# Moving v's projections to the end of a half step, with a query-key projection in their place

## The chip, the cores and the metric

The kernel runs on one core of a Trainium2 chip. TensorE (PE) does the matrix products and the transposes, VectorE (DVE), ScalarE (ACT) and GpSimd (POOL) the elementwise work, and SyncE (SP) issues nearly all DMA transfers. The metric is the time of one execution in microseconds (us), as the device counts it; the median of three runs before the change is 3634.91 us (3633.56 to 3640.62).

## The reference: what is computed

The input is 16 sequences of 256 tokens with 128 features, in float32. First comes one causal attention layer with 16 heads of 8 features, added to its input. Then come six layers, and what they make is added too:

```python
for i in range(DEPTH):                       # 6
    x = attn_layer(shift_tokens(x), ...) + x # 16 heads of 64, windows of 32
    x = ffn_layer(shift_tokens(x), ...) + x  # layernorm, W1, a * gelu(gate), W2
```

`shift_tokens` moves half of the features one token on. `attn_layer` projects to q, k and v (1024 features each), divides q and k by their lengths per head, scales and rotates them by position, and lets each window of 32 queries attend to its own and the previous window, with a mask. The output is projected back to 128 features.

## The kernel before, in words

A first stage (up to about 390 us) does the causal attention; it is not touched. The second stage, lines 378 to 863, does the six layers and takes the rest.

The unit of the second stage is one sequence in one layer, n = 0 to 95 (six layers of 16 sequences; sequence n % 16). Every n is done in two **half steps**, `half(n, u)` with u = 0 and 1, and a half step mixes the work of several n, so that the engines have something to do while others finish:

- for n + 2: `shift` and the projections to q and k, `proj_qk(n + 2, g, k)`, for four groups g of heads, with k = 0 for q and 1 for k. In half u the groups are i = 2u and j = 2u + 1. Each projection is a pair of products on PE (name `qk`), a square on ACT (line 486, `sq`), a product with the position tables on DVE (line 487, `t`); after k = 1, three additions on POOL (lines 496 and 499, `sq` and `tq`).
- for n + 1: the lengths of q and k. In u = 0 `norms` sums the squares on PE (`n`), `roots` transposes them (`nT`) and takes the reciprocal root on DVE in a chain of small operations (lines 521 to 530, `nx`, `rn`, `nz`), and POOL spreads the result (line 533, `kb`). `spread_k` transposes kb on PE (line 544, `bc`), `norm_k` multiplies k with it on DVE (line 558, `tq`), and four DMAs on SP put q and k in place (`us`); both for two groups in u = 0 and two in u = 1.
- for n: `masks` and `sim` put the masked scores into PSUM (lines 585 and 605), `soften` scales them and subtracts their maximum (DVE `sm`, `mx`, POOL line 626), `power` takes the exponential (ACT line 632).
- for n (u = 1) or n - 1 (u = 0), the blocks bi and bj: `share` divides by the sum (DVE `rec`, POOL or DVE line 642), `attn_T` transposes the weights on PE (line 648, `aT`) with a copy on ACT, `attn_v` multiplies them with v in 64 small products on PE (line 668, `po`) with a copy on ACT (line 677, `ao`). `project_out` of n - 1 is `wo`.
- v: `proj_v(n, u, c)` projects the half c of the tokens for the heads of u: one product on PE (line 568, recorded as two), a copy on ACT (line 574, `vn`), and transfers on SP that lay v out a window further on (`vs`): two for c = 0 (lines 575 and 577), one for c = 1. It is read by `attn_v` in the half step that follows. On a layer's first sequence `load_v` fetches the weights.
- for the pair m of two sequences: the feed-forward part, spread over the half steps. In **odd n, u = 0** `glu_center` takes off the mean (PE `cen`, ACT line 709 `fsq` and line 711 `xc`) and `glu_var` sums the squares (PE line 718, `pv`, which reads fsq); in **odd n, u = 1** come `glu_norm` and two of three `glu_part` (PE `hg`, `ha`, ACT line 753, DVE line 755); in **even n, u = 0** the third; in **even n, u = 1** `glu_out` (PE `w`).

So there are four kinds of half steps, and a cycle of four repeats 48 times.

PSUM has four single buffers for all of this (`psum1`: qk, n, nT, aT, v, cen, pv, hg, ha, bc, wo, w take them in turn) and two double ones (`psum2`, for sim and po). A product waits until the earlier tenant of its buffer has been read.

The order of the work is the order in which the code calls it. `in_order` (line 89) ties every instruction of PE, DVE, ACT and POOL to the one before it on its engine; only SP's transfers are placed by the scheduler. Each engine then works through its queue in that order, and waits by semaphores where an input or a buffer isn't ready.

## Time and profile before

| | us |
|---|---|
| median of three runs | 3634.91 (3633.56 to 3640.62) |
| the profiled execution | 3631.49, of which the span is 3629.4 |
| PE busy | 3485.9 (96%), at a mean granted clock of 0.992 |
| DVE busy | 2841.1 (78%) |
| POOL busy | 2592.8 (71%) |
| ACT busy | 1870.2 (52%) |
| PE's share of the chain that ended last | 76% |

The profile is one execution. A line of a timeline gives the start in us from the span's start, the duration, the engine, the line of the code, the operation, what it writes and reads, how many instructions are merged in the row, and in brackets the idle time of the engine before it with what ended it. A line of the waits gives the engine and line that waited, for whom, the total, how often, and the longest. Two times are told apart by subtracting starts: on PE the end of a product is modelled and overlaps the next start, so the step from one start to the next is what counts.

### The profile page before, as it was taken

What the parts mean: (1) busy time and instruction counts of PE and PEld (TensorE: products, weight loads), DVE (VectorE), ACT (ScalarE), POOL (GpSimd) and SP (SyncE); (2) the same over time, 40 slices, a digit from 0 to 9 for tenths busy, and PEclk for the clock granted to TensorE, in tenths of its full rate; (3) what the DMA queues carried; (4) which work ended last, traced back from release to release, by engine and by line L of the source; (5) the groups of instructions that cost most, each with busy time, mean ns of one, the idle gap of its engine ahead of it and who ended that gap; (6) DMA issues with size and microseconds to landing.
All of it is one profiled execution on the core that took longest, in us unless ns stands there. A gap on an engine that the chain in (4) does not pass through costs nothing.

```text
span 3629.4 us, 153727 instructions
## 1 busy us (share of the span) xinstructions
PE 3485.9 (96%) x68032; PEld 2451.9 (68%) x68032; DVE 2841.1 (78%) x4866; ACT 1870.2 (52%) x3132; POOL 2592.8 (71%) x2731
## 2 busy tenths in 40 slices
PE   7999799999999999999999999999999999999998
PEld 5777466666666666666666666666676666666665
DVE  5765788887888888888877888877888888888784
ACT  2444355554555555555555555555555555555453
POOL 2221778778777778787777777778777877777772
PEclk9999899999999999999999999999999999999999
DMA  2000333334433334333334433334433343333342
GB/s 82 8 10 10 94 91 100 100 88 110 111 102 84 96 100 111 102 104 100 88 92 117 107 88 99 100 86 116 111 95 83 100 111 93 102 105 102 90 105 60
DMA packets 249444, 331.65 MB, mean 91 GB/s; under 512 B 74446, under 2 KB 105548, under 8 KB 247884
## 3 DMA queue, kind: packets, MB, share of 16 engines
q1 hardware_dynamic: 248060, 321.13, 33.1%
q8 instruction: 536, 8.78, 1.0%
q14 instruction: 128, 1.05, 0.1%
q10 hardware_dynamic: 720, 0.70, 0.1%
HBM read 28.12 MB, written 4.19 MB: 9 GB/s over the span
## 4 chain that ended last, share of the span: by engine, by line
PE 76%; DVE 9%; issue 7%; POOL 3%; ACT 2%; DMA 1%; SPq 0%; POOLq 0%; DVEq 0%; ACTq 0%
PE qk L485 17%; PE po L668 11%; PE v L568 9%; PE wo L688 8%; PE sim L605 6%; PE w L764 4%; PE hg L750 3%; PE ha L751 3%; PE aT L648 3%; PE n L506 2%; DVE tq L558 2%; DVE t L487 2%; PE bc L544 2%; PE sim L585 2%; ACT aT L650 1%
## 5 line engine op out<-in xcount | busy, mean ns | idle before, releaser
L487 DVE TENSOR_TENSOR t<-qk,ab 128x1024 f32<-128x1024 f32 x768 | 915.9, 1218 | 284.1 <-ACT sq L486 252.4
L499 POOL TENSOR_TENSOR tq<-t 128x512 f32<-128x512 f32 x768 | 962.1, 1274 | 85.4 <-DVE t L487 61.0
L485 PE MATMUL qk<-xs,wqk 128*128 128x256 f32 x3072 | 790.9, 393 | 1.6 <-DVE yT L693 1.5
L496 POOL TENSOR_TENSOR sq<-sq 128x512 f32<-128x512 f32 x384 | 489.1, 1274 | 282.3 <-ACT sq L486 272.3
L485 PEld LDWEIGHTS qk<-xs,wqk 128*128 128x128 f32 x3072 | 555.3, 191 | 146.9 <-issue 45.5
L486 ACT ACTIVATE sq<-qk 128x512 f32<-128x512 f32 x768 | 459.4, 599 | 377.3 <-PE qk L485 371.3
L650 ACT COPY aT<-aT 128x512 f32<-128x512 f32 x384 | 207.6, 587 | 599.4 <-PE aT L648 599.2
L668 PEld LDWEIGHTS po<-aT,vs 64*64 64x64 f32 x12288 | 327.8, 135 | 201.2 <-issue 106.8
L568 PE MATMUL v<-wv,xs 128*128 128x512 f32 x768 | 423.8, 634 | 28.1 <-ACT aT L650 21.2
L626 POOL TENSOR_TENSOR sm<-sm,mx 128x512 f32<-128x512 f32 x384 | 396.6, 1045 | 28.1 <-DVE mx L625 27.2
L605 PEld LDWEIGHTS sim<-us 64*32 64x32 f32 x24576 | 260.7, 105 | 205.9 <-issue 189.1
L668 PE MATMUL po<-aT,vs 64*64 64x32 f32 x12288 | 394.6, 222 | 5.2 <-issue 2.6
L668 PE MATMUL po<-aT,vn 64*64 64x32 f32 x12288 | 386.8, 219 | 4.6 <-issue 4.6
L574 ACT COPY vn<-v 128x512 f32<-128x512 f32 x384 | 225.3, 587 | 312.8 <-PE v L568 308.7
L688 PE MATMUL wo<-ao,wout 128*128 128x256 f32 x1536 | 383.2, 392 | 1.0 <-ACT ao L677 1.0
L642 POOL TENSOR_TENSOR ex<-ex,rec 128x512 f32<-128x512 f32 x288 | 317.5, 1116 | 39.7 <-ACT vn L574 18.2
L668 PEld LDWEIGHTS po<-aT,vn 64*64 64x64 f32 x12288 | 330.2, 136 | 5.1 <-issue 4.9
L605 PE MATMUL sim<-us 64*32 64x64 f32 (+1 forms) x24576 | 322.9, 221 | 3.1 <-DMA us<-tq 3.1
L688 PEld LDWEIGHTS wo<-ao,wout 128*128 128x128 f32 x1536 | 276.0, 189 | 49.5 <-ACT ao L677 1.7
L677 ACT COPY ao<-po 128x512 f32<-128x512 f32 x384 | 222.7, 580 | 114.9 <-PE po L668 114.9
L639 DVE TENSOR_REDUCE rec<-ex 128x8 f32<-128x512 f32 x384 | 252.0, 657 | 34.2 <-ACT ex L632 34.2
L625 DVE TENSOR_REDUCE mx<-sm 128x8 f32<-128x512 f32 x384 | 263.5, 686 | 13.3
(122 smaller groups left out, 5244.7 us busy)
## 6 DMA issues: line engine op xcount, KB each, us to landing
us<-tq SPq DMA_DIRECT2D x768, 256.0 KB
vs<-vn SPq DMA_DIRECT2D x384, 192.0 KB
vs<-vn SPq DMA_DIRECT2D x192, 64.0 KB
wqk<-in_f_wqkv_dram SPq DMA_DIRECT2D x96, 64.0 KB
ab<-in_tables_dram SPq DMA_DIRECT2D x6, 1024.0 KB
wv<-in_f_wqkv_dram SPq DMA_DIRECT2D x12, 256.0 KB
wout<-in_f_wo_dram SPq DMA_DIRECT2D x24, 128.0 KB
x<-in_x_dram SPq DMA_DIRECT2D x16, 128.0 KB
```

The lines of the kernel that those rows point to most:

```text
L485: nc.tensor.matmul(ps[:, t * S : t * S + S], W["qk", g][:, k, t, :], xs[n], start=True, stop=True)
L486: nc.scalar.activation(sq2[:, k].rearrange("p t n -> p (t n)"), ps, AF.Square)
L487: nc.vector.tensor_tensor(t12[:, k].rearrange("p f t n -> p f (t n)"), ps.unsqueeze(1).to_broadcast([P, 2, 2 * S]), W["ab", l][:, k].rearr ...
L496: nc.gpsimd.tensor_tensor(sq[n, g], sq2[:, :, 0, :], sq2[:, :, 1, :], ALU.add)
L499: nc.gpsimd.tensor_tensor(tq[n, g][:, t], t12[:, :, 0, t, :], t12[:, :, 1, 1 - t, :], ALU.add)
L568: nc.tensor.matmul(ps, xs[n][:, P * c : P * c + P], W["v"][:, u].rearrange("p g x d -> p (g x d)"), start=True, stop=True)
L605: nc.tensor.matmul(ps[WIN * r : WIN * r + WIN, x, col + first : col + 64], qk[part, g, 0, WIN * c : WIN * c + WIN], qk[part, g, 1, WIN * ( ...
L625: nc.vector.tensor_reduce(mx, seg, AX.X, ALU.max)
L626: nc.gpsimd.tensor_tensor(seg, seg, mx.unsqueeze(2).to_broadcast([P, 8, 64]), ALU.subtract)
L642: on.tensor_tensor(seg, seg, rec.unsqueeze(2).to_broadcast([P, 8, 64]), ALU.mult)
L668: nc.tensor.matmul(po[DH * y : DH * y + DH, h, x, g, WIN * r : WIN * r + WIN], v[64 * h : 64 * h + 64, r // 2, 2 * g + y, x, :], aT[64 * h ...
L688: nc.tensor.matmul(ps[:, :S].rearrange("p (h m) -> p h m", h=2), W["out"][:, g, 2 * u + x, :], a[:, x, :, g, :], start=(j == 0), stop=(j == 3)
```

## The change

Two calls in `half` change places. The first piece of v, `proj_v(n, u, 0)`, stood between the transposes `attn_T` and the values `attn_v(b, bi)`; it now stands at the end of the half step, directly ahead of the second piece. Where it stood, there is now the q projection of the second group, `proj_qk(n + 2, j, 0)`, which stood after `attn_v(b, bi)` (and in odd n, u = 0 after `glu_center`). Nothing is added or left out.

```diff
             do(b, attn_T, bi)
             do(b, attn_T, bj)
-            do(n, proj_v, u, 0)
+            do(n + 2, proj_qk, j, 0)
             do(b, attn_v, bi)
             if not even and u == 0 and glu(m):
                 glu_center(m)
-            do(n + 2, proj_qk, j, 0)
             if even and u == 0 and glu(m - 1):
                 glu_part(m - 1, 2)
...
                     leave(2 * ((m - 1) % 8))
                     leave(2 * ((m - 1) % 8) + 1)
+            do(n, proj_v, u, 0)
             do(n, proj_v, u, 1)
```

## The prediction

> **What bounds the kernel now.** I read the page's busy line first, then the stretches of 600 us, the waits of PE, and the timeline of each engine over one cycle of four half steps (2061 to 2127 us). Half steps (n, u) come in four kinds: u = 0 or 1, n even or odd.

> ```profile
> PE 3485.9 (96%) x68032; PEld 2451.9 (68%) x68032; DVE 2841.1 (78%) x4866; ACT 1870.2 (52%) x3132; POOL 2592.8 (71%) x2731
> ```
> ```profile
> 1450.00:2050.00 600.00, 590.61 (x11562) 411.86 (x11561) 489.76 (x812) 322.62 (x531) 470.94 (x490) 1.00 0.38 101
> ```

> In the long middle PE (first figure after 600.00) is busy 590.6 of 600 us at granted clock 1.00; DVE, ACT and POOL have 18%, 46% and 22% idle. PE takes its queue in order, so the time is PE's work plus each place where its next instruction is not ready. A cycle is 65.9 us. The change leaves PE the same instructions; only gaps can change. What gaps there are stand in the waits (us in total, times, longest):

> ```profile
> PE v L568 <- ACT aT L650: 21.2, 89, 0.2
> PE v L568 <- DVE tq L558: 6.1, 33, 0.4
> ```

> Now the two u = 0 kinds, from the timelines (start, duration, engine, line, idle before). Even n, PE, then DVE, then POOL:

> ```profile
> 2069.11 1.12 PE L568 MATMUL v<-wv,xs 128*128 128x512 f32 x2 [0.24 <-ACT aT L650]
> 2070.17 0.32 PE L668 MATMUL po<-aT,vs 64*64 64x32 f32 x8
> ...
> 2071.23 1.13 PE L485 MATMUL qk<-xs,wqk 128*128 128x256 f32 x4
> 2072.20 1.02 PE L750 MATMUL hg<-xn,w 128*85 128x512 f32 x2
> 2073.06 1.02 PE L751 MATMUL ha<-xn,w 128*85 128x512 f32 x2
> 2073.91 1.03 PE L485 MATMUL qk<-xs,wqk 128*128 128x256 f32 x4
> 2074.78 0.60 PE L544 MATMUL bc<-cst,kb 128*128 128x128 f32 x4
> ```
> ```profile
> 2063.96 2.36 DVE L487 TENSOR_TENSOR t<-qk,ab 128x1024 f32<-128x1024 f32 x2 [0.71 <-ACT sq L486]
> ...
> 2070.25 1.00 DVE L528 TENSOR_TENSOR nz<-nx,rn 128x64 f32<-128x64 f32 x1
> ```
> ```profile
> 2066.64 2.52 POOL L499 TENSOR_TENSOR tq<-t 128x512 f32<-128x512 f32 x2
> 2069.10 2.07 POOL L626 TENSOR_TENSOR sm<-sm,mx 128x512 f32<-128x512 f32 x2
> 2073.45 1.04 POOL L533 COPY kb<-rn 128x1024 f32<-128x1024 f32 x1 [2.29 <-DVE rn L530]
> ```

> bc reads kb, which POOL finishes at 2074.49; PE comes to bc at 2074.78. The slack is 0.29 us, hidden by work ahead of it. Odd n, PE, ACT, DVE and POOL:

> ```profile
> 2103.67 1.13 PE L707 MATMUL cen<-x,cst 128*128 128x512 f32 x2
> 2104.64 1.03 PE L485 MATMUL qk<-xs,wqk 128*128 128x256 f32 x4
> 2105.50 1.04 PE L718 MATMUL pv<-cst,fsq 128*128 128x1 f32 x8
> 2106.40 1.11 PE L485 MATMUL qk<-xs,wqk 128*128 128x256 f32 x4
> 2107.35 0.60 PE L544 MATMUL bc<-cst,kb 128*128 128x128 f32 x4
> ```
> ```profile
> 2104.84 0.60 ACT L709 ACTIVATE fsq<-cen 128x512 f32<-128x512 f32 x1 [0.44 <-PE cen L707]
> ```
> ```profile
> 2096.46 2.36 DVE L487 TENSOR_TENSOR t<-qk,ab 128x1024 f32<-128x1024 f32 x2 [1.08 <-ACT sq L486]
> ```
> ```profile
> 2105.70 1.04 POOL L533 COPY kb<-rn 128x1024 f32<-128x1024 f32 x1 [2.29 <-PE qk L485]
> ```

> pv reads fsq, which ends at 2105.44, and starts at 2105.50: the qk between cen and pv fills exactly the time of ACT's square. kb has 0.61 us of slack here (2106.74 against 2107.35).

> **The change, part by part.**

> *The projection qk(j,0) takes v's place after the transposes.* Its four matmuls go ahead of the 64 of attn_v(bi), on ACT its square ahead of the copy ao and, in odd u = 0, of fsq and xc; on DVE its t meets nothing new. It waits, as v did, for the first aT copy, so the 0.24 us stay. Price there: v to po is 1.06 us (2069.11 to 2070.17); qk is a matmul of the same pitch (0.86), so 1.06 again: nothing. At a layer's start its weight loads pass vs's transfers on SP, which makes them earlier.

> *Odd u = 0: qk leaves the place between cen and pv.* cen stays at 2103.67, fsq at 2104.84 to 2105.44, pv at 2105.50; PE stands idle for the 0.86 us that qk took. Behind pv are queued qk(j,1), bc, attn_v(bj), the masks and the next half. ACT is free for fsq (it waited 0.44 us for cen). So nothing becomes earlier, and v is added at the end of the half: v before another full matmul 0.97 (like qk to hg after po), the second v 0.95 (2092.81 to 2093.76 in even u = 1) in place of 1.05 (2109.28 to 2110.33): +0.87. The weight load that qk covered may now show for up to 0.1. I take 0.92 (bounds 0.75, if fsq comes 0.1 earlier, and 1.06) in the 46 odd steps that hold cen and a projection: 42.3 us.

> *Even u = 0: v leaves the stretch before bc.* PE would reach bc at 2069.11 + 1.06 + 1.06 + 0.97 + 0.86 + 0.86 = 2073.92. kb cannot follow: it ends a chain on DVE and POOL that starts with t at 2063.96, and that t waited 0.71 us for the square of a projection at the half's head, which does not move. One part can: DVE's first nz takes 1.00 us where the next two take 0.22, and ends at 2071.25, 0.08 after POOL's subtraction (2071.17); in odd n the two ends are 2103.48 and 2103.41. POOL's tq before it could start 0.2 earlier (t ends 2066.32, tq starts 2066.64 behind POOL's own queue, which the earlier projection of the half before shortens). So kb at 2074.29, bc at 2074.35: 0.43 earlier than now, v 0.87 at the end, 0.1 for a weight load no longer covered: +0.54. Bounds: 0.2 (kb 0.5 earlier) and 0.86 (kb unmoved, 0.63, and switches of 0.1 twice). 42 steps: 22.7 us. I take the value nearer the middle because both halves' rows tie nz's end to POOL's.

> [...]

> *Odd u = 1.* PE's order becomes qk, po, hg, ha, hg, ha, qk. ACT's first gelu ends at 2123.23; its table load began when the square was done and moves up some 1.1 us with qk, so the later qk, which needs its PSUM place, does not wait. v's two copies on ACT stand ahead of the next half's square: 0.59 more, covered by that same 1.1 us; without it the next square would be 0.32 late (0.27 idle before it now). Price 0.

> *Even u = 1.* attn_v(bj) now has one projection (0.96) between it and attn_v(bi), whose ao copy ends 0.73 after PE leaves it (2086.80 to 2087.53): no wait. The v that waited 0.18 us for DVE's tq becomes a qk that waits for the same; PE comes there later than DVE does now: the 6.1 us of the second wait line go.

> *v's transfers.* c = 0's two now stand on SP behind us's four (u = 0) and ahead of c = 1's: the last starts about 1.1 to 1.9 us later than 2080.64, and attn_v needs it at about 2086.3. The trace shows no landing; it shows no wait with 5.1 us and leaves about 3.5. Bounds 0 and 1 us at 94 steps; I take 0, since this stretch uses 0.62 of the DMA engines. v's weights (load_v), asked for on SP before the last vs of the half ahead, are needed only at the half's end: nothing.

> *Edges.* First and last even steps have kb with 0.05 of slack: 2 × 0.9. At five layer starts POOL's tables (L427) hold everything; POOL's queue ahead of them is 1.1 us earlier, against v's 0.87: 5 × -0.25.

> Sum: 42.3 + 22.7 - 6.1 + 1.8 - 1.3 = 59.4 us. The profiled execution took 3631.5 (span 3629.4), so 3690.9; the runs' median is 3.4 above it, so **3694**.

> **The rivals.**

> *Only pv's gap opens (0.12).* POOL and DVE run ahead far enough that kb comes 0.5 us earlier: 42.3 - 6.1 + 0.5 gives 3672. For it: the 22% that POOL has idle. Against: DVE waits for PE (0.71) at the chain's head.

> *Both gaps at their upper bounds (0.16).* 46 × 1.06 + 42 × 0.86 + 1.8 = 87 us and no gain: 3722. [...]

> *Transfers late (0.05).* 0.5 us at 94 steps more: 3741. For it: 0.62 of the DMA engines in that stretch; against: 3.5 us of room.

> *Not slower (0.05).* PE's records are pipelined and their ends modelled; if DVE's queue paces the halves (it runs without idle time from 2075.75 to 2087.53) and PE only looks full, v at the end and the gap before pv lie in PE's slack, and even u = 1's wait goes: 3629. It decides where DVE has less idle time at a half's head than the gap is long; the rows say 0.71 and 1.08, against 0.43 and 0.86.

> **How the numbers follow.** Main case 0.62 (3681 to 3708 by itself). 3668 to 3724 holds it, the first two rivals but their edges, some 0.87. A measurement here tells 0.2% (7 us) from nothing: slower 0.95; same 0.03 and faster 0.02 come from the last rival, whose 3629 lies near the edge.

> **What would show it.** After: a wait of PE pv on ACT fsq of 0.8 to 0.9 us some 46 times; PE bc on POOL kb of about 0.4, some 42 times; "v <- ACT aT" turned into "qk <- ACT aT", still 0.24; "<- DVE tq" gone; the cycle 67.2 us. Wrong if pv starts less than 1.7 us after cen, if kb ends more than 0.5 us earlier in its half, or if po waits for vs.

## The result, and the profile after

The changed kernel takes 3699.51 us (median of 4 executions, 3698.94 to 3701.81) against 3635.19 us before: a ratio of 1.0179, 95% interval 1.0166 to 1.0192, or 64 us more. The profiled execution took 3699.42 (span 3697.5) against 3631.49. The forecast was 3694.

The busy line of the page, and the stretch of the long middle that was shown of before:

```profile
PE 3508.1 (95%) x68032; PEld 2457.5 (66%) x68032; DVE 2845.4 (77%) x4866; ACT 1874.5 (51%) x3132; POOL 2577.3 (70%) x2731
```
```profile
1450.00:2050.00 600.00, 581.75 (x11324) 403.59 (x11323) 481.01 (x799) 318.57 (x522) 459.05 (x475) 0.99 0.36 97
```

PE has the same 68032 instructions. Its idle time is 45.9 us longer (span less busy time: 143.5 before, 189.4 after), but its busy time has grown too, by 22.2 us, and the granted clock of the stretch reads 0.99 where it read 1.00; over the whole span it is 0.986 against 0.992. Gaps alone do not do that. First the gaps, in the waits of PE (us in total, times, longest), after and then before:

```profile
PE bc L544 <- POOL kb L533: 36.5, 49, 5.4
PE pv L718 <- ACT fsq L709: 33.0, 48, 0.7
...
PE qk L485 <- ACT aT L650: 20.9, 88, 0.2
```
```profile
PE bc L544 <- POOL kb L533: 16.5, 11, 5.2
...
PE pv L718 <- ACT fsq L709: 1.4, 2, 0.7
```

pv now waits for ACT's square in every odd n, bc for POOL's kb in every even n, the 0.24 us behind the transposes have only changed owner, and no line "<- DVE tq" is left. The timelines of the half steps that were shown of before; odd n, u = 0, PE and ACT:

```profile
2139.88 1.12 PE L707 MATMUL cen<-x,cst 128*128 128x512 f32 x2
2141.69 1.05 PE L718 MATMUL pv<-cst,fsq 128*128 128x1 f32 x8 [0.69 <-ACT fsq L709]
2142.61 1.11 PE L485 MATMUL qk<-xs,wqk 128*128 128x256 f32 x4
2143.55 0.60 PE L544 MATMUL bc<-cst,kb 128*128 128x128 f32 x4
```
```profile
2141.04 0.60 ACT L709 ACTIVATE fsq<-cen 128x512 f32<-128x512 f32 x1 [0.44 <-PE cen L707]
```

From cen to pv it is 1.81 us, before 1.83: the projection that stood between them is gone, and pv starts no earlier. Even n, u = 0, PE, DVE and POOL:

```profile
2105.29 1.13 PE L485 MATMUL qk<-xs,wqk 128*128 128x256 f32 x4 [0.24 <-ACT aT L650]
2106.35 0.32 PE L668 MATMUL po<-aT,vs 64*64 64x32 f32 x8
...
2107.42 1.09 PE L750 MATMUL hg<-xn,w 128*85 128x512 f32 x2
2108.34 1.02 PE L751 MATMUL ha<-xn,w 128*85 128x512 f32 x2
2109.20 1.03 PE L485 MATMUL qk<-xs,wqk 128*128 128x256 f32 x4
2110.51 0.63 PE L544 MATMUL bc<-cst,kb 128*128 128x128 f32 x4 [0.28 <-POOL kb L533]
```
```profile
2106.16 1.00 DVE L528 TENSOR_TENSOR nz<-nx,rn 128x64 f32<-128x64 f32 x1
```
```profile
2105.03 2.05 POOL L626 TENSOR_TENSOR sm<-sm,mx 128x512 f32<-128x512 f32 x2
2109.37 1.04 POOL L533 COPY kb<-rn 128x1024 f32<-128x1024 f32 x1 [2.29 <-PE ha L751]
```

Counted from the first matmul behind the transposes, kb ends 5.12 us on (before 5.38) and bc starts 5.22 us on (before 5.67).

To see what each half step costs, I took PE's timeline between 560 and 3300 us and measured, for every half step, from its first wo (L688) to its masks (L585), and from there to the next wo; medians over some 41 of each kind, in us:

| half step | before: to the masks + behind them | after | difference |
|---|---|---|---|
| odd n, u = 0 | 10.71 + 5.73 | 10.72 + 6.59 | +0.87 |
| odd n, u = 1 | 11.16 + 5.85 | 10.29 + 6.71 | -0.01 |
| even n, u = 0 | 10.59 + 5.29 | 10.17 + 6.15 | +0.44 |
| even n, u = 1 | 8.13 + 8.43 | 6.86 + 9.29 | -0.41 |
| cycle | 65.89 | 66.78 | +0.89 |

Behind the masks each half step has v's first piece more, 0.86 us. Ahead of them it has one matmul less, and only odd n, u = 1 gives all 0.86 back. The cycle's 0.89 us in some 47 cycles are 42 us, not 64. The rest is the clock. Four microseconds to a line, the columns being length, busy time of PE, PEld, DVE, ACT and POOL, granted clock, DMA share and GB/s; the changed kernel, and then a second execution of it at the same place:

```profile
1528.00:1532.00 4.00, 3.31 (x75) 2.11 (x73) 3.69 (x11) 2.26 (x4) 1.71 (x3) 1.00 0.02 4
1532.00:1536.00 4.00, 4.00 (x53) 3.21 (x56) 1.77 (x3) 1.63 (x3) 2.72 (x3) 0.57 0.00 0
1536.00:1540.00 4.00, 4.00 (x114) 2.36 (x108) 3.90 (x8) 1.76 (x3) 3.71 (x4) 1.00 0.49 119
```
```profile
1532.00:1536.00 4.00, 3.31 (x57) 2.64 (x56) 2.45 (x8) 1.97 (x4) 2.28 (x3) 1.00 0.00 0
1536.00:1540.00 4.00, 4.00 (x118) 2.38 (x111) 3.90 (x8) 2.39 (x5) 4.00 (x4) 1.00 0.30 61
```

In the first execution pv's 0.69 us of idle time (pv starts at 1531.40) is followed by 3.4 us at half clock: 0.43 of 4 us are lost, 1.7 us (the half step is 1.6 us longer). In the second the same pv (1533.04) has the same idle time, and the clock stays. Adding up (1 - clock) x 4 us over all such windows between 600 and 3400 us, the kernel before loses 3.3 us, the changed one 15.3 and in its second execution 20.5. Between 437 and 645 us, where the second stage starts, it is 1.7 against 8.5. Together some 19 us. pv is not behind all of this: of the first execution's eight stretches between 600 and 3400 us three stand behind pv, three behind bc's wait at a layer's start (2.2 us, before 1.3) and two behind waits without a cause that the profile shows; in the second execution these are seven, three and two.

### The profile page after: what moved, and what is told of

It is laid out like the page before. It is cut to its first block, busy times and chain, and to the rows that moved or that the text cites. A ratio compares the mean times of both kernels' runs of the same rounds, so it can differ in the third digit from the quotient of the medians.

```text
span 3697.5 us, 153690 instructions
## 1 busy us (share of the span) xinstructions
PE 3508.1 (95%) x68032; PEld 2457.5 (66%) x68032; DVE 2845.4 (77%) x4866; ACT 1874.5 (51%) x3132; POOL 2577.3 (70%) x2731
## 3 DMA queue, kind: packets, MB, share of 16 engines
q14 instruction: 127, 1.04, 0.1%
## 4 chain that ended last, share of the span: by engine, by line
PE 81%; issue 6%; DVE 4%; POOL 4%; ACT 3%; DMA 2%; SPq 0%; POOLq 0%; DVEq 0%; ACTq 0%
PE qk L485 18%; PE po L668 11%; PE v L568 10%; PE wo L688 9%; PE sim L605 8%; PE w L764 4%; PE hg L750 4%; PE aT L648 3%; PE ha L751 3%; PE bc L544 2%; PE n L506 2%; PE sim L585 2%; ACT aT L650 1%; PE cen L707 1%; POOL kb L533 1%
## 5 line engine op out<-in xcount | busy, mean ns | idle before, releaser
L487 DVE TENSOR_TENSOR t<-qk,ab 128x1024 f32<-128x1024 f32 x768 | 919.8, 1218 | 342.7 <-ACT sq L486 312.2
L499 POOL TENSOR_TENSOR tq<-t 128x512 f32<-128x512 f32 x768 | 961.6, 1273 | 73.1 <-DVE t L487 70.9
L485 PE MATMUL qk<-xs,wqk 128*128 128x256 f32 x3072 | 801.8, 394 | 21.1 <-ACT aT L650 20.9
L486 ACT ACTIVATE sq<-qk 128x512 f32<-128x512 f32 x768 | 458.7, 598 | 500.0 <-PE qk L485 484.2
L485 PEld LDWEIGHTS qk<-xs,wqk 128*128 128x128 f32 x3072 | 548.8, 191 | 159.4 <-issue 45.5
L650 ACT COPY aT<-aT 128x512 f32<-128x512 f32 x384 | 207.6, 587 | 594.3 <-PE aT L648 594.1
L626 POOL TENSOR_TENSOR sm<-sm,mx 128x512 f32<-128x512 f32 x384 | 396.6, 1043 | 35.8 <-DVE mx L625 34.9
L668 PEld LDWEIGHTS po<-aT,vs 64*64 64x64 f32 x12288 | 329.7, 135 | 123.5 <-issue 64.0
L668 PE MATMUL po<-aT,vs 64*64 64x32 f32 x12288 | 396.8, 223 | 8.5 <-DMA vs<-vn 4.3
L668 PE MATMUL po<-aT,vn 64*64 64x32 f32 x12288 | 389.2, 220 | 3.6 <-issue 3.6
L568 PE MATMUL v<-wv,xs 128*128 128x512 f32 x768 | 386.5, 627 | 0.0
L688 PE MATMUL wo<-ao,wout 128*128 128x256 f32 x1536 | 383.2, 392 | 0.2 <-ACT ao L677 0.2
L668 PEld LDWEIGHTS po<-aT,vn 64*64 64x64 f32 x12288 | 332.3, 136 | 3.4 <-issue 3.4
L642 POOL TENSOR_TENSOR ex<-ex,rec 128x512 f32<-128x512 f32 x288 | 296.4, 1043 | 31.9 <-ACT vn L574 13.8
L688 PEld LDWEIGHTS wo<-ao,wout 128*128 128x128 f32 x1536 | 276.0, 189 | 48.6 <-ACT ao L677 0.8
```

Source lines behind the costliest of these rows:

```text
L485: nc.tensor.matmul(ps[:, t * S : t * S + S], W["qk", g][:, k, t, :], xs[n], start=True, stop=True)
L486: nc.scalar.activation(sq2[:, k].rearrange("p t n -> p (t n)"), ps, AF.Square)
L487: nc.vector.tensor_tensor(t12[:, k].rearrange("p f t n -> p f (t n)"), ps.unsqueeze(1).to_broadcast([P, 2, 2 * S]), W["ab", l][:, k].rearr ...
L499: nc.gpsimd.tensor_tensor(tq[n, g][:, t], t12[:, :, 0, t, :], t12[:, :, 1, 1 - t, :], ALU.add)
L568: nc.tensor.matmul(ps, xs[n][:, P * c : P * c + P], W["v"][:, u].rearrange("p g x d -> p (g x d)"), start=True, stop=True)
L626: nc.gpsimd.tensor_tensor(seg, seg, mx.unsqueeze(2).to_broadcast([P, 8, 64]), ALU.subtract)
```

## The experiments

All ratios are to the kernel before on the same chip. The ratio is of medians; what stands behind it is read from one trace of each kernel: the cycle as above, and the time lost at half clock between 600 and 3400 us with the number of stretches whose longest idle time nearby is pv's.

| kernel | ratio (95%) | cycle, us | lost at half clock, us | behind pv |
|---|---|---|---|---|
| before, shown / again | | 65.89 / 65.89 | 3.3 / 1.7 | 0 / 0 |
| changed, shown / again | 1.0179 (1.0166-1.0192) | 66.78 / 66.78 | 15.3 / 20.5 | 3 / 7 |
| u = 1 only | 1.0028 (1.0017-1.0039) | 65.89 | 5.1 | 0 |
| odd n, u = 0 only | 1.0153 (1.0134-1.0172) | 66.74 | 18.7 | 6 |
| even n, u = 0 only | 1.0052 (1.0032-1.0073) | 66.17 | 15.4 | 0 |
| changed, cen earlier | 1.0105 (1.0082-1.0128) | 66.27 | 6.9 | 0 |
| places swapped in u = 0 | 1.0185 (1.0168-1.0202) | 66.92 | 11.8 | 0 |
| changed, half a subtraction | 1.0153 (1.0132-1.0175) | 66.52 | 13.6 | 4 |
| changed, qk between the transposes | 1.0128 (1.0108-1.0147) | 66.37 | 11.9 | 2 |
| before, v between the transposes | 0.9893 (0.9875-0.9910) | 65.07 | 3.3 | 0 |

### The change in one kind of half step alone

```diff
             do(b, attn_T, bj)
-            do(n + 2, proj_qk, j, 0)
+            new = u == 1            # the others: u == 0 and not even; u == 0 and even
+            do(*((n + 2, proj_qk, j, 0) if new else (n, proj_v, u, 0)))
             do(b, attn_v, bi)
             if not even and u == 0 and glu(m):
                 glu_center(m)
+            if not new:
+                do(n + 2, proj_qk, j, 0)
...
-            do(n, proj_v, u, 0)
+            if new:
+                do(n, proj_v, u, 0)
             do(n, proj_v, u, 1)
```

> The change in the half steps with u = 1 alone; u = 0 as before. Prediction's reasons: odd u = 1 costs 0, even u = 1 gains the 6.1 us of the wait v <- DVE tq, and both of u = 0's gaps stay closed (pv <- fsq 1.4 us, bc <- kb 16.5 us in total, as before): 0.998 of before, some 6 us less. Rival 'transfers late' in the u = 1 half of its places: 0.5 us at 47 places, 1.005, with waits of po on vs. Rival 'v's two copies on ACT hold up the next half's square': 0.32 us at 46 places, 1.004.

Measured: 3646.49 us against 3638.79. No time was gained: the wait for tq only has a new owner, and the cycle is the one before. In this version's waits:

```profile
PE po L668 <- issue: 12.6, 7, 2.5
PE qk L485 <- DVE tq L558: 7.2, 38, 0.4
...
PE sim L585 <- issue: 5.3, 3, 1.9
```

The 8 us that it is slower are not in the cycle. Waits without a cause that the profile shows ("issue") are 18.9 us behind 460 us, against 10.4 in the trace before.

> The change in the u = 0 half steps of odd n alone. Prediction: pv waits for fsq 46 times and nothing of it is given back: +42.3 us, 1.0116. By the changed kernel's trace, where this wait is 0.69 us (33.0 us in 48 times): +33 us, 1.009, and more than that where the granted clock of TensorE falls to half behind the gap; how much more is the number to be learnt. Rival (the gap hides in slack of PE's modelled busy time): 1.000.

Measured: 3692.1, 53 us more. The wait of pv is 33.0 us in 48 times, as in the changed kernel, and the half step is 0.87 us longer. 47 cycles of 0.85 are 40 us, and 15 us more are lost at half clock (18.7 against 3.3): 55. Six of its ten stretches at half clock stand right behind pv, four of them in the consecutive cycles at 988, 1056, 1124 and 1192 us. The other four stand at layers' starts, behind two waits of 0.9 us that the kernel before has as well.

> The change in the u = 0 half steps of even n alone. Prediction: bc waits for kb, 0.54 us a step in 42 steps, and 1.8 at the edges: +24.5 us, 1.0067. By the changed kernel's trace (bc <- kb 36.5 us against 16.5): +20 us, 1.0055. Rival 'only pv's gap opens': 0 or 0.5 us a step earlier, 1.000. pv <- fsq stays at 1.4 us.

Measured: 3655.43, 17 us more. bc waits in every even n, and with 0.54 us (median) where it is 0.29 in the changed kernel:

```profile
PE bc L544 <- POOL kb L533: 46.7, 50, 6.0
```

Its even half step u = 0 is 0.70 us longer, and the half step behind it 0.42 shorter although nothing was changed there: PE comes to tq late enough that the wait is gone. So the shortening of even u = 1 belongs to u = 0's delay, not to u = 1's new order, in which the first version found no gain.

The two versions also show where kb's earlier end comes from. Counted from the first matmul behind the transposes (medians), kb ends at 5.37 us here, as in the kernel before, and at 5.12 in the u = 1 version, as in the changed kernel; POOL's tq ahead of it ends 0.25 us earlier there. So it is the new order of the half step ahead, odd u = 1, that brings kb forward. Of this version's seven stretches at half clock five stand behind bc's wait at a layer's start; the traced execution was the longest of the four (3662).

### Taking pv's gap away

```diff
             do(n + 2, proj_qk, j, 0)
-            do(b, attn_v, bi)
             if not even and u == 0 and glu(m):
                 glu_center(m)
+            do(b, attn_v, bi)
```

> The changed kernel with the GLU's cen matmul ahead of attn_v(bi), so that attn_v's 0.97 us stand between cen and pv. Prediction (pv's gap is ACT's square alone, and it alone costs the odd steps): the 33 us of pv <- fsq go and 33 to 42 us with them: 3657 to 3667 us, 1.006 to 1.009 of before. If the stretches at half clock in the changed kernel (11 more of some 3.4 us than before) are set off by pv's gap too, their share of about 19 us goes as well: down to 1.002. Rival: PE waits elsewhere for the same ACT work (ao or the next square), 1.018 as the changed kernel.

Measured: 3675.71 (3665.26 in the profiled execution). pv no longer waits, but PE now comes early to the next thing that is not ready, bc in odd n, which waits 0.22 us there:

```profile
PE bc L544 <- POOL kb L533: 48.7, 95, 6.0
```

So the half step gets 0.51 of its 0.87 us back, and the loss at half clock falls to 6.9 us with no stretch behind pv. The profiled execution lies in the range that was named for the gap alone (3657 to 3667); the median is 9 us above it, and the further gain by the clock is not seen in the time, though it is in the trace.

### Giving the cover back with another matmul

```diff
             do(b, attn_v, bi)
             if not even and u == 0 and glu(m):
                 glu_center(m)
+            if u == 0:
+                do(n, proj_v, u, 0)
...
-            do(n, proj_v, u, 0)
+            if u:
+                do(n, proj_v, u, 0)
             do(n, proj_v, u, 1)
```

> In u = 0 the two matmul groups only change places: qk(j,0) stands after the transposes as in the changed kernel, v's first piece stands where qk(j,0) was (between cen and pv in odd n, ahead of hg in even n). u = 1 as in the changed kernel. Theory: the loss of the change is the cover that u = 0 lost, whatever matmul gives it: pv <- fsq back to 1.4, bc <- kb to some 16, cycle 65.9, time 1.000 to 1.003 of before. Rival: what costs is qk(j,0)'s place or v's two pieces on ACT and SP: 1.005 or more.

Measured: 3702.25 against 3634.94, as slow as the change. Both old gaps are closed (pv waits once, bc 10.8 us in all), but a new one takes their place:

```profile
PE qk L485 <- DVE t L487: 28.5, 91, 2.1
```

In the program, qk(j,1) here waits for t of qk(j,0): it is given the PSUM buffer that qk(j,0) had. That t stands on DVE behind the whole chain of roots (in this trace it runs from 2079.77 to 2080.99, and qk(j,1) starts at 2081.04 with 0.21 us idle). In the kernel before, the matmul at this early place was v, which ACT copies out at once (v from 2069.11, its copy from 2070.27 to 2070.86). So my theory holds only in part: the lost cover is what costs, but not any matmul can give it: with qk(j,0) here, PE waited 28.5 us in all for the engine that reads its buffer. A further 0.32 us are in odd u = 1: qk behind the transposes has the buffer that DVE's xn (line 739) reads, and starts 0.05 us after xn ends (2092.26 and 2092.31), where in the changed kernel it starts 0.20 after it (2154.24 and 2154.44); DVE runs later there, without idle time from 2082.84 to 2096.36.

### What holds kb

```diff
-            nc.gpsimd.tensor_tensor(seg, seg, mx.unsqueeze(2).to_broadcast([P, 8, 64]), ALU.subtract)
+            k = 4 if i == 1 else 8
+            nc.gpsimd.tensor_tensor(
+                seg[:, :k], seg[:, :k], mx[:, :k].unsqueeze(2).to_broadcast([P, k, 64]), ALU.subtract
+            )
```

> The changed kernel with POOL's second subtraction (L626, i = 1) done for 4 of its 8 segments only: half of one softmax's shift is left out. If DVE's first nz lasts 1.00 us because it is held until that subtraction ends, then both end 0.5 us earlier, kb with them, and bc <- kb of the even half step (0.29 us in the middle of the run) goes: 36.5 falls by 12 to 15 us. In time 0 to 15 us less than the changed kernel, since the half step after it (even u = 1) was shorter by as much as PE came later. Rival: 1.00 us is nz's own cost: kb and the wait do not move.

This version leaves out half of one softmax's shift. Measured: 3687.59. DVE and POOL, an odd n, and two waits of PE (the edit moves the later lines by three):

```profile
2166.90 0.57 DVE L528 TENSOR_TENSOR nz<-nx,rn 128x64 f32<-128x64 f32 x1
```
```profile
2165.78 1.61 POOL L627 TENSOR_TENSOR sm<-sm,mx 128x512 f32<-128x512 f32 x2
```
```profile
PE pv L721 <- ACT fsq L712: 33.0, 48, 0.7
PE bc L544 <- POOL kb L533: 21.0, 11, 5.6
```

nz ends 0.08 us after the subtraction again (2167.47 and 2167.39), but lasts 0.57 instead of 1.00. In the changed kernel the first nz lasted 1.00 us and ended 0.07 to 0.10 us after POOL's subtraction in 91 of 96 half steps; in this version it lasted 0.57 and ended as close behind it in 92. In four half steps of the changed kernel no instruction of POOL ran beside nz, and it lasted 0.23 us. bc's wait is down by 15.5 us, to what it is at the layers' starts; the even half step u = 0 is 0.42 us shorter, the one behind it 0.16 longer. So nz ends with POOL's subtraction, at its full length and at the shorter one; what in the hardware ties the two ends together is not shown.

### The 0.24 us behind the transposes

In the kernel before (and, with qk(j,0) for v, in the changed kernel):

```diff
             do(b, attn_T, bi)
+            if u == 0:
+                do(n, proj_v, u, 0)
             do(b, attn_T, bj)
-            do(n, proj_v, u, 0)
+            if u:
+                do(n, proj_v, u, 0)
```

> The kernel before with one edit of the opposite kind: in u = 0, v's first piece stands between the two transposes instead of behind them. The 0.24 us for the first aT copy (21.2 us in 89 times) are then covered by v's 0.86 us. If kb keeps its slack (0.29 and 0.61), 88 times 0.24: -21 us, 0.994. If the even half step's kb and its successor's wait for tq give part of it back (tq's wait grows by what PE comes earlier): -10 us, 0.997. Rival: the second transpose now waits for the same copy: 1.000.

Measured: 3595.06 us, 40 us less than before; this beats both kernels. PE's timeline, odd n:

```profile
2083.76 0.60 PE L648 MATMUL aT<-cst,ex 128*128 128x128 f32 x4
2084.20 1.02 PE L568 MATMUL v<-wv,xs 128*128 128x512 f32 x2
2085.13 0.63 PE L648 MATMUL aT<-cst,ex 128*128 128x128 f32 x4
```

Nothing waits any more between the transposes and the values. The odd half step u = 0 is 0.40 us shorter, not 0.24, the even one 0.15 (bc there starts 0.11 us after kb ends, as it does where it waits), and even u = 1 0.27, where the wait for tq is gone as well: 0.82 us a cycle, 47 times, is 39 us. Its time at half clock is that of the kernel before.

> The changed kernel with one more edit: in u = 0, qk(j,0) stands between the two transposes, so that PE no longer stands 0.24 us behind them. By the gaps: odd n 0.24 to 0.40 us a cycle less; in even n PE only comes to kb sooner and waits there (bc <- kb from 0.29 to 0.5 us), 0: cycle 66.4 to 66.5 against 66.8, 11 to 18 us under the changed kernel, 1.013 to 1.015 of before. By the clock: in three of the changed kernel's and six of the odd-only version's cycles the clock fell to half right behind pv's 0.69 us with the 0.24 us some 4 us ahead of it. If it takes both idle times in one stretch of 3.4 us, these dips go, and 5 us more. Rival (the two kernels differ only by what covers the 0.24 us, as when v stood there in the kernel before): -39 us, 1.007.

Measured: 3681.11, some 18 us under the changed kernel. In odd n 0.41 us are gone, in even n none: bc now waits 0.70 us instead of 0.29, and the cycle is 66.37.

```profile
PE bc L544 <- POOL kb L533: 54.0, 49, 6.1
PE pv L718 <- ACT fsq L709: 33.0, 48, 0.7
```

Two stretches at half clock still stand behind pv, without the 0.24 us ahead of it. So pv's gap does not need the other; that part of the expectation falls. And idle time alone does not do it: none of the 35 short waits of bc (median 0.70 us) between 600 and 3400 us was followed by half clock.

### Two kernels once more

> The kernel before once more, for its trace on the chip of these experiments: a cycle of four half steps 65.9 us, pv <- fsq 1.4, bc <- kb some 16. What is asked of it: how much the waits without a named cause ('issue', 10.4 us in the trace shown) and the time at half clock differ from one execution to another, since the u = 1 version came out 8 us over before with the same cycle of 65.9 us.

Measured: 3639.15 us, the same cycle; "issue" waits of 13.1 us against 10.4, 1.7 us at half clock. The issue waits thus differ by some us between executions of one kernel, which covers only part of the u = 1 version's 8 us. From the first wo to the last this trace takes 3171.9 us, the shown one of the same kernel 3164.5 and the u = 1 version 3170.8, so the traces do not show where the medians' 8 us lie; that stays open.

> The changed kernel once more, for a second trace: the same cycle of 66.8 us and the same waits (pv <- fsq 33, bc <- kb some 36). [...]

Measured: 3700.43, the same waits (bc 36.6, pv 33.0). Seven stretches at half clock stand behind pv, at 1190 and 1260 us for instance, and none at the cycles of 1532 and 1600, where the first execution has two. So the instruction does not decide it.

## Why the forecast was right, and where not

3694 was forecast and 3699.5 measured, but that it is so near is luck: the gaps cost some 42 us where 59.4 were forecast (the cycle came to 66.78 us, not 67.2), and the clock, which was not in the sum, adds about 19.

| step | forecast, us | measured |
|---|---|---|
| odd u = 0, pv's gap | 46 x 0.92 = 42.3 | 46 x 0.87 = 40 |
| even u = 0, bc's gap | 42 x 0.54 = 22.7 | 42 x 0.44 = 18.5 |
| odd u = 1 | 0 | 0 |
| even u = 1, wait for tq gone | -6.1 | 42 x -0.41 = -17 |
| edges | +1.8 - 1.3 = 0.5 | not measured apart |
| clock | not in the sum | about +19 |

- *qk(j,0) in v's place* costs nothing, as said: 1.06 us to po, the wait of 0.24 unchanged.
- *Odd u = 0* went as described: cen to pv unmoved, v at the end. The 0.05 us that I added for a weight load are not there: cen to pv is 1.81 us, before 1.83, and pv's weight load is recorded from pv's own start on (2141.69). The wait reads 0.69 us, not the 0.8 to 0.9 that I named; the loss is 0.87 all the same (below).
- *Even u = 0* is right in its mechanism: kb came 0.26 us earlier (0.2 forecast), through POOL's subtraction and the half step ahead as argued, and bc 0.45 earlier (0.43). The 0.1 for a weight load was again too much: bc's load is recorded from 2110.48, 0.03 us ahead of bc.
- *Even u = 1* is the mis-sized term. I priced the wait at its row, 0.18 us 33 times. PE's two starts before and after:

```profile
2083.49 1.04 PE L648 MATMUL aT<-cst,ex 128*128 128x128 f32 x8
2084.71 1.10 PE L568 MATMUL v<-wv,xs 128*128 128x512 f32 x2 [0.18 <-DVE tq L558]
```
```profile
2120.12 1.04 PE L648 MATMUL aT<-cst,ex 128*128 128x128 f32 x8
2120.99 1.03 PE L485 MATMUL qk<-xs,wqk 128*128 128x256 f32 x4
```

  From start to start 1.22 us became 0.87: the wait cost 0.35, and the half step 0.41. The reason that I gave for its going (PE comes later) is the right one; the even-only version shows it without any change in u = 1.
- *v's transfers*: waits of po on vs are 1.5 and 3.8 us in two traces of the kernel before, 4.3 and 3.6 in two of the changed one: no rise that stands out of the scatter, and I took 0.
- *The missing step* is the clock. I read 1.00 in the long middle and took PE's busy time as fixed. The new idle times set off stretches at half clock, 12 us more between 600 and 3400 us and 7 at the start of the second stage. That pv's gap does a part of this is shown by the version without it (no stretch behind pv) and by the odd-only version (six). Another part stands behind bc's longer wait at the layers' starts (three stretches in either execution; five in the even-only version).

From 631 us of the kernel before to the last wo, the changed kernel loses 56.3 us: 44.75 cycles of 0.89 are 39.8, the clock 12, and 4.5 are left that I do not attribute; the two traces of the kernel before differ by 7.3 over the same stretch. The rivals fell: both gaps opened; neither reached its upper bound; transfers stayed hidden; and the modelled ends of PE hid no slack.

## What to carry to other kernels

Price a wait of PE by the step from one start to the next, not by the idle time in its row (here 0.69 us in the row cost 0.87). Before moving a matmul out of a place, ask which other engine's work its time covers (here the 0.60 us of ACT's square) and when the engine that reads it gives the buffer back (DVE's t held qk for 28.5 us in 91 waits); a gap of under a microsecond may then also cost clock, as pv's 0.69 us did in 3 and 7 of 41 cycles. And the place worth filling was the one that already had a wait, between two transposes: 0.24 us in the row, and 40 us less in all.

## What the runs showed of the hardware that I had not expected

- An idle row understates a wait on PE by 0.15 to 0.18 us, since the record before it ends some 0.16 us after the point at which the next product starts where nothing waits (above, ha's record of 1.02 us from 2108.34 ends 0.16 us after the start of the qk behind it, 2109.20): 0.69 in the row cost 0.87 (pv), 0.24 cost 0.40 (transposes), 0.29 cost 0.44 and 0.54 cost 0.70 (bc in the changed kernel and in the even-only one), 0.18 cost 0.35 (tq).
- An idle time of 0.69 us in a PE that is otherwise full can be followed by 3.4 us at half clock, which costs 1.7 us; it came 3 and 7 times of 41 in two executions of the same kernel, at different cycles, and over five traces exactly where the idle time began 1.64 to 1.91 us ahead of a point of the grid of 3.413 us. Within the same step of the grid lie also pv's own eight products of one column, and none of 35 idle times ahead of bc (median 0.70 us) was followed by half clock: how much the products count was not tested.
